# A planned GNN and mixture-of-experts kernel: layer 3's batch statistics three tiles later, layer 2's PSUM copies on ScalarE, and slack in the planner behind TensorE's products

## The chip, the cores and the metric

The kernel runs on one core of one Trainium2 chip. The metric is the device time of one execution in microseconds, as the median of three runs. A profile is one further execution, recorded by the hardware profiler. The engines are named TensorE (PE, and PEld for its weight loads), VectorE (DVE), ScalarE (ACT), GpSimd (POOL) and SyncE (SP, which issues DMAs). Each engine has its own queue of instructions and takes them in order, so an instruction that waits holds up everything behind it on that engine.

## The reference, cut to what matters

The input x has 3125 nodes with 256 features; 50,000 edges are sorted by their target node. Four times a graph layer and a feed-forward layer are added to x, each on a layer norm of x. The change touches the layers with index 2 and 3.

```python
# layer 2, graph: attention over the edges into a node
z = h @ W_func.T                       # e from z[src], z[dst], w; softmax over a node's edges
h_new = h @ W_self.T + segment_sum(alpha[:, None] * z[edge_src], edge_dst)
out = h + relu(where(deg > 0, h_new, h))
# layer 2, feed-forward: 16 experts, 256 -> 512 -> 256, the best two for each node
topk_vals, topk_idx = top_k(x @ gate_w + gate_b, 2)
moe = sum(softmax(topk_vals) * expert_out[topk_idx]);  layer norm of x + moe
# layer 3, graph: maximum over the edges (and the node itself), then batch norm
xp  = relu(x @ W_proj.T + b_proj)
agg = segment_max(xp[src], dst)
out = relu(agg @ W_l.T + b_l + x @ W_r.T)
mean, var = out.mean(axis=0), out.var(axis=0)   # over all 3125 nodes
out = (out - mean) * rsqrt(var + 1e-5) * gamma + beta
# layer 3, feed-forward: 8 experts, 256 -> 512 -> 256, the best two for each node
```

## The kernel before, in words

All is float32. Nodes lie in 25 tiles of 128 rows, sorted so that tile 0 holds the nodes with most incoming edges; tile t needs RND[t] rounds (line 70: 32, 24, 22, ... down to 9, in all 413), and in each round every one of its nodes takes one neighbour. A round is one indirect DMA on GpSimd's queue (`gather`, line 136), which fetches 128 rows of a table in HBM by index. Routed rows go back to HBM with an indirect DMA of the same kind (`scatter`, line 140).

**Layer 2** runs in one stretch whose order is not the order of the code. Several Python generators ("chains") each yield their next step as (engine, estimated us, what it needs); class `Plan` (line 1693) keeps an estimated time at which each engine is free, and always issues the step that can start first, by rank where several are within 0.05 us. A step's result counts as there after its estimate and a delay of its engine (TensorE 0.35, VectorE 0.13, ScalarE 0.2, GpSimd 2.4 us). Where a step names two engines, the one that can start first takes it, ScalarE on a tie. The plan fixes the order of instructions on each engine for good; on the chip semaphores alone decide when each starts. The chains are:

- `gathers` (line 2214): per tile one gather of the tile's own rows (XX) and RND[t] of neighbour rows (g_rows, blocks of 4 rows, 9 blocks in a ring).
- `attend` (2229): per tile a transpose and a product pu on TensorE (one PSUM buffer), a copy a_xt on ScalarE, on VectorE the scores g_e, on ScalarE their exponential (2261), on VectorE the sum g_dn and its reciprocal (2263 to 2266), the first accumulation with pu (2268), and one multiply-add for each gathered row (2273), which frees the block.
- `route2` (2281): for six groups of tiles the layer norm (ScalarE), a transpose and a copy r_xt (`logit_steps`, 1818, from `turned_steps`, 1761: either engine), the router's product and its sum r_lg on VectorE (1832), then `Experts.route` (1883): the best two, counts by a product (1904), positions, two scatters per tile to xg, and the experts' output bias as a product from a copied ro_ct (1969) added to a base row in ACC (1976).
- `tokens`, `weights` (1988, 2000): SyncE's loads of an expert's rows and its weights, two buffers each.
- `experts2` (2290), which runs `Experts.run` (2021) for three chunks of tiles (CH2, line 76: tiles 15 to 24, 6 to 14, 0 to 5), 16 experts each, at the lowest rank: rows are transposed and copied from PSUM as ro_xt (2045, either engine), multiplied with W1 (1982), passed through the activation to ro_h on ScalarE (2063), multiplied with W2 (1986), and copied from PSUM as ro_y (2080, either engine).

The first `pl.run` (2338) ends when all groups are routed. Then the remaining experts run beside `fetch` and `table3` (2294), which combine the experts' rows, norm them and write layer 3's table tab3.

**Layer 3's graph part** has an order written by hand (from line 2388). GpSimd's gathers run 24 rows ahead (ROWS). For each tile t, TensorE transposes x to g_xt (copied by ScalarE, line 1653); VectorE takes RND[t] maxima into ACC (2395), and after each issues the gather of the row 24 further on; then TensorE transposes the result (g_at, copied by ScalarE), two pairs of products (2405, 2407) give the two halves of the tile's output, and ScalarE's Relu puts them into Y (2408). Two `bn_stats` on VectorE (`stats`, 2384) take a tile's contribution to the batch norm:

```python
if t and r == OFF[t] + 6:
    stats(t - 1)
```

that is, the statistics of the tile before stand behind the seventh maximum of the present tile, and those of the last tile behind the loop. Layer 3's feed-forward part is planned again, in the manner of layer 2, with its own `Experts`.

Of the kernel before, what the change touches and what calls it, by code (L numbers as in the profile page):

```python
# [21 lines left out]
NT = 25  # L22
# [15 lines left out]
GT = 5  # L38
MM_COL = 0.0019
# [31 lines left out]
OFF = [sum(RND[:t]) for t in range(NT + 1)]  # L71
# [24 lines left out]
def tile_gnn_ffn(ctx: ExitStack, tc: tile.TileContext, a: dict, out: bass.AP):  # L96
# [1686 lines left out]
    plan = [None]  # L1783
# [34 lines left out]
    def logit_steps(lg, src, g, w, b, n, ready, R, pool, name, us, *args, **kw):  # L1818

        last = None  # L1820
        for i in range(g + 1):
            if i < g:
                xt = pool.tile([P, 2, P], F32, name=name, bufs=2)
                xf = yield from turned_steps(R["tp"], xt, src[:, i, :], ready[i], us, *args, **kw)
            if i:
                f = yield "PE", 0.4, (last[1], R["u"])
                free = R["u"].take()
                pl_ = ps("u", [P, 2, D])[:, 0, :n]
                for k in range(2):
                    nc.tensor.matmul(pl_, last[0][:, k, :], w[:, k, :], start=(k == 0), stop=(k == 1))  # L1830
                f = yield "DVE", 0.08, (f,)
                nc.vector.tensor_add(lg[:, i - 1, :], pl_, b)
                free.t = f
            last = (xt, xf)
        return f
# [8 lines left out]
    class Experts:  # L1844
# [3 lines left out]
        def __init__(self, key, n, act, chunks, pool, xg, yg, scale=None, bias=None):  # L1848
            self.n, self.act, self.chunks, self.pool, self.xg, self.yg = n, act, chunks, pool, xg, yg
            self.scale, self.bias = scale, bias  # L1850
# [32 lines left out]
        def route(self, c, t0, g, lg, f, residual, R, pre="ro_"):  # L1883
# [25 lines left out]
            f = yield "DVE", 0.16, (f,)  # L1909
# [44 lines left out]
            there = f  # L1954
            last = None
            for t in range(t0, t0 + g):
# [10 lines left out]
                f = yield ("ACT", "DVE"), 0.25, (f,)  # L1967
# [7 lines left out]
                f = yield "DVE", 0.33, (f,)  # L1975
# [45 lines left out]
        def run(self, c, R):  # L2021
# [4 lines left out]
            def turn(e):  # L2026
# [5 lines left out]
                for q in range(2):  # L2032
                    f = yield "PE", 0.13 * k, (xl, R["tp"])
                    free = R["tp"].take()
                    pt = ps("tp", [P, 512])
                    for i in range(k):
                        nc.tensor.transpose(pt[:, i * m : (i + 1) * m], x[:, i, q * P : (q + 1) * P], ident[:m, :m])  # L2037
                    if q:
                        xfree.t = f
                    f = yield ("ACT" if self.scale is not None else ("ACT", "DVE")), 0.15 + cols * 0.0011, (f,)  # L2040
                    if self.scale is not None:
                        nc.scalar.activation(xt[:, q, :], pt[:, :cols], AF.Identity, bias=self.bias[:, q : q + 1],  # L2042
                                             scale=self.scale[:, q : q + 1])
                    else:
                        (nc.scalar.copy if plan[0].on == "ACT" else nc.vector.tensor_copy)(xt[:, q, :], pt[:, :cols])
                    free.t = f
# [3 lines left out]
            for e in range(self.n):  # L2050
# [18 lines left out]
                for i0 in range(0, k, 2):  # L2069
# [9 lines left out]
                    f = yield ("ACT", "DVE"), 0.15 + 0.27 * g, (f,)  # L2079
# [70 lines left out]
    with tc.tile_pool(name="g2", bufs=2) as gp, \  # L2150
# [130 lines left out]
        def route2():  # L2281
            for c, t0, g in ((0, 20, 5), (0, 15, 5), (1, 10, 5), (1, 6, 4), (2, 0, 4), (2, 4, 2)):
                s = slice(t0, t0 + g)
                ready = yield from norm_steps(XN[:, s, :], X[:, s, :], g, gp, "rn_", [done[t] for t in range(t0, t0 + g)])
                lg = wp.tile([P, GT, 16], F32, name="r_lg")
                f = yield from logit_steps(lg, XN[:, s, :], g, rw2, gb2, 16, ready, R, gp, "r_xt", 0.36, which=("ACT", "DVE"))
# [43 lines left out]
        with tc.manual_schedule(engines={EN.PE, EN.DVE, EN.Activation, EN.Pool, EN.SP}):  # L2330
# [5 lines left out]
                                   .rearrange("p r d -> p (r d)"), here[order2[-1]])))  # L2336
            last = pl.add(4, experts2())
            pl.run(moved, R.values())
            ex2.rest(range(NT))
# [11 lines left out]
    with tc.tile_pool(name="w3", bufs=1) as wp:  # L2351
# [9 lines left out]
        with tc.tile_pool(name="g3", bufs=2) as gp, psums(tp=3, mm=4):  # L2361
# [25 lines left out]
            with tc.manual_schedule(engines={EN.PE, EN.DVE, EN.Activation, EN.Pool, EN.SP}):  # L2387
                for r in range(ROWS):
                    look(r)
                for t in range(NT):  # L2390
# [3 lines left out]
                    for r in range(OFF[t], OFF[t + 1]):  # L2394
                        nc.vector.tensor_tensor(u, u, rows.pop(r), op=OP.max)  # L2395
                        look(r + ROWS)
                        if t and r == OFF[t] + 6:
                            stats(t - 1)
# [10 lines left out]
                stats(NT - 1)  # L2409
# [131 lines left out]
```

## Time and profile before

| What | us |
|---|---|
| median of 3 runs (4182.8 to 4201.5) | 4183.03 |
| the profiled execution's own time | 4229.5 |
| its span, first to last instruction | 4227.7 |
| layers 0 and 1, up to layer 2's first gather | 0 to 2074 |
| layer 2's gathers, attention, routing and experts | 2074 to 2940 |
| layer 2's last experts, norms and tab3 | 2940 to 3179 |
| layer 3's gathers, maxima and statistics | 3179 to 3784 |
| layer 3's feed-forward part | 3784 to 4228 |
| TensorE, VectorE, ScalarE, GpSimd busy in the whole span | 2697.7, 1946.6, 845.3, 1758.5 |

Stages are cut by hand where the instructions of the next begin; all times inside the span are of the one profiled execution. Busy time is the sum of the instructions' records. "Waited for" puts the idle time in front of an instruction down to the event that ended it: an instruction, a DMA, "issue" where the profile shows nothing that was waited for, "remote" where the source is not known. A tile's name stands without buffer numbers: `ro_xt<-tp` is the copy that fills ro_xt from PSUM's tp.

### The profile page before, as it was taken

The numbers are of one execution on the slowest core, as the hardware profiler recorded it, in microseconds if no ns is written. First come the engines' busy times: TensorE is split into PE (matmuls) and PEld (weight loads), VectorE is DVE, ScalarE is ACT, GpSimd is POOL, SyncE is SP. The second block draws the span as 40 slices with busy tenths as digits, with TensorE's granted clock in tenths as the row PEclk, the third lists the DMA queues.
The fourth block names the chain that finished last, engine by engine and source line by source line (L and its number), as shares of the span: only waits on it lengthen the run. The fifth ranks groups of instructions, "written<-read, shape, count | busy, mean of one in ns | idle before, by whom it ended". The sixth has DMA issues, their size and how long they took to land. (4 is left out here: it accounts for less than half of the span.)

```text
span 4227.7 us, 46661 instructions
## 1 busy us (share of the span) xinstructions
PE 2697.7 (64%) x12940; PEld 2134.4 (50%) x12940; DVE 1946.6 (46%) x7501; ACT 845.3 (20%) x1803; POOL 1758.5 (42%) x1996
## 2 busy tenths in 40 slices
PE   1688999989889999948411365365670112137875
PEld 0566878767677878737310254254550111125653
DVE  3445666665665555442344333444662233245300
ACT  1112232221122222211100021122220000013322
POOL 4342333341253333002466544544437666643323
PEclk9878999999799999968755576577775555566987
DMA  7766455452243444113233254365523333323543
GB/s 223 223 190 187 129 157 144 130 154 65 76 118 107 118 133 126 52 48 107 73 93 91 86 175 141 107 185 168 174 90 101 87 92 88 92 81 107 158 159 100
DMA packets 275971, 521.46 MB, mean 123 GB/s; under 512 B 53609, under 2 KB 176897, under 8 KB 275685
## 3 DMA queue, kind: packets, MB, share of 16 engines
q0 software_dynamic: 105344, 306.57, 25.0%
q1 hardware_dynamic: 159598, 201.27, 15.6%
q10 hardware_dynamic: 10742, 10.34, 0.8%
q8 instruction: 114, 1.87, 0.2%
q14 instruction: 173, 1.41, 0.1%
HBM read 431.19 MB, written 86.78 MB: 123 GB/s over the span
## 5 line engine op out<-in xcount | busy, mean ns | idle before, releaser
L136 POOL DMA_INDIRECT g<-tab,m_si x521 | 498.0, 956 | 989.9 <-DVE mt L890 526.5
L136 POOL DMA_INDIRECT g_rows<-tab,srcI x413 | 401.9, 973 | 300.4 <-DVE ACC L2273 157.3
L136 POOL DMA_INDIRECT g_row<-tab,srcI x413 | 400.4, 970 | 196.3 <-issue 104.6
L880 PEld LDWEIGHTS c<-s,g 128*128 128x128 f32 x2084 | 345.8, 217 | 166.7 <-issue 83.9
L880 PE MATMUL c<-s,g 128*128 128x96 f32 x2084 | 356.1, 299 | 100.1 <-issue 38.2
L887 PE MATMUL pw<-w_d,f 65*128 65x256 f32 x1042 | 374.4, 445 | 14.2 <-DVE mt L890 11.9
L919 PE MATMUL f<-w_rel,aT 128*126 128x256 f32 x1600 | 372.6, 383 | 0.1
L884 ACT COPY aT<-c 128x384 f32<-128x384 f32 (+1 forms) x323 | 237.1, 737 | 595.7 <-PE c L880 397.5
L1982 PE MATMUL mm<-ro_xt,ro_w 128*128 128x192 f32 (+3 forms) x928 | 255.9, 428 | 122.3 <-ACT ro_h L2063 73.1
L919 PEld LDWEIGHTS f<-w_rel,aT 128*126 128x126 f32 x1600 | 300.2, 190 | 50.5 <-issue 5.3
L1651 PE MATMUL tp<-ident,ACC 128*128 128x128 f32 x50 | 16.1, 424 | 462.5 <-DVE ACC L2395 357.2
L890 DVE TENSOR_TENSOR mt<-pw,g 128x256 f32<-128x256 f32 x521 | 218.7, 420 | 159.0 <-PE pw L887 83.8
L1986 PE MATMUL y<-ro_w,ro_h 128*96 128x256 f32 (+2 forms) x1040 | 263.6, 409 | 33.5 <-ACT ro_h L2063 19.1
L1982 PEld LDWEIGHTS mm<-ro_xt,ro_w 128*128 128x128 f32 x928 | 183.8, 221 | 178.4 <-ACT ro_h L2063 80.5
L1651 PEld LDWEIGHTS tp<-ident,ACC 128*128 128x128 f32 x50 | 7.1, 199 | 470.5 <-issue 441.1
L1986 PEld LDWEIGHTS y<-ro_w,ro_h 128*96 128x96 f32 (+2 forms) x1040 | 190.4, 189 | 86.9 <-ACT ro_h L2063 23.1
L1037 PE MATMUL w<-w,b_h 128*126 128x256 f32 x800 | 218.5, 398 | 11.1 <-ACT xt L950 3.0
L1028 PE MATMUL w<-xt,w 128*128 128x252 f32 (+1 forms) x832 | 221.3, 392 | 6.3 <-issue 3.4
L140 POOL DMA_INDIRECT xg<-XX,ro_pos x100 | 101.6, 1016 | 287.6 <-issue 136.5
L2273 DVE SCALAR_TENSOR_TENSOR ACC<-g_rows,g_e,ACC 128x256 f32<-128x256 f32 x413 | 200.9, 486 | 43.9 <-DVE ACC L2273 19.9
L2395 DVE TENSOR_TENSOR ACC<-ACC,g_row 128x256 f32<-128x256 f32 x413 | 173.2, 424 | 67.1 <-DMA g_row<-tab,srcI 48.0
L2240 PE MATMUL pu<-w_s,a_xt 128*128 128x256 f32 x100 | 45.9, 606 | 231.5 <-DVE ACC L2268 104.8
(580 smaller groups left out, 4791.0 us busy)
## 6 DMA issues: line engine op xcount, KB each, us to landing
ro_w<-in_L_ffn_blocks SPq DMA_DIRECT2D x58, 514.0 KB
ro_w<-in_L_ffn_blocks SPq DMA_DIRECT2D x58, 512.0 KB
f<-in_attr_t SPq DMA_DIRECT2D x521, 32.5 KB
xg<-zero SPq DMA_DIRECT2D x78, 200.0 KB
b_at<-in_edge_attr SPq DMA_DIRECT2D x100, 125.0 KB
tabr<-v SPq DMA_DIRECT2D x12, 758.0 KB
g<-tab,m_si POOLq DMA_INDIRECT x521
g_rows<-in_L_ffn_blocks SPq DMA_DIRECT2D x14, 514.0 KB
```

The costliest lines, as they stand in the source:

```text
L136: return nc.gpsimd.indirect_dma_start(out=dst, out_offset=None, in_=table, in_offset=bass.IndirectOffsetOnAxis(ap=idx, axis=0))
L880: nc.tensor.matmul(pc[:, h, o : o + GW], g[:, h * P : (h + 1) * P], sums[k][0], start=True, stop=True)
L884: nc.scalar.copy(aT[:, :, :, b : b + n * GN].rearrange("p k r n -> p k n r"), pc[:, :, : n * GW].rearrange("p k (n r) -> p k n r", r=16))
L887: nc.tensor.matmul(pw, feats.pop(k), wd, start=True, stop=True)
L890: nc.vector.tensor_tensor(mt[0], pw, rows.pop(k)[:, D:], op=OP.mult)
L919: nc.tensor.matmul(cur["f"][:TN], aT[:, h, r, :], wrel[:, h, r, :], start=(r == 0 and h == 0), stop=(r == 15 and h == 1))
L1028: nc.tensor.matmul(ph, w["01"][:, e, k, i * P : (i + 1) * P], xt[:, k, : n * TN], start=(k == 0), stop=(k == 1))
L1037: nc.tensor.matmul(py, last[:, k, i * TN : (i + 1) * TN], w["02"][:, e - 1, k, :], start=(k == 0), stop=(k == 1))
L1982: nc.tensor.matmul(ph, w[:, o : o + P], xt[:, k, :], start=(k == 0), stop=(k == 1))
L1986: nc.tensor.matmul(py, h[:, i, s], w[:, i * D : (i + 1) * D], start=(i == 0), stop=(i == self.fc - 1))
L2273: stt(u, g[:, r, :D], e[:, r0 + r : r0 + r + 1], u, op0=OP.mult, op1=OP.add)
L2395: nc.vector.tensor_tensor(u, u, rows.pop(r), op=OP.max)
```

## The change

It has four parts. In layer 3 the statistics of tile t - 3 (LATE) take the place of those of tile t - 1, and those of the last three tiles stand behind the loop. In layer 2, while the first plan runs, `Experts.out` is ScalarE alone, so the copies ro_xt, ro_ct and ro_y that either engine could take have only ScalarE; after that plan both are allowed again. The copies r_xt of layer 2's router are ScalarE's alone too, through the default of `turned_steps`. And for the groups of chunks 0 and 1 the planner counts 3 us more (SLACK) until a product of TensorE is there for a VectorE step of the routing (the sum r_lg, the positions, the base rows), and 1.5 us more before the scatters; the yielded steps themselves are unchanged. No arithmetic is added or taken away.

```diff
--- before.py
+++ after.py
@@ -36,6 +36,8 @@
 ROWS = 24
 W_BUFS = 2
 GT = 5
+LATE = 3
+SLACK = 3.0
 MM_COL = 0.0019
 KEEP = max(1, N // 2) - 1
 KB = -(-KEEP // P)
@@ -1780,7 +1782,7 @@
         free.t = f
         return f
 
-    plan = [None]
+    plan, slack = [None], [0.0]
 
     def norm_steps(dst, src, n, pool, pre, ready, twice=False, which=("ACT",)):
 
@@ -1828,7 +1830,7 @@
                 pl_ = ps("u", [P, 2, D])[:, 0, :n]
                 for k in range(2):
                     nc.tensor.matmul(pl_, last[0][:, k, :], w[:, k, :], start=(k == 0), stop=(k == 1))
-                f = yield "DVE", 0.08, (f,)
+                f = yield "DVE", 0.08, (f + slack[0],)
                 nc.vector.tensor_add(lg[:, i - 1, :], pl_, b)
                 free.t = f
             last = (xt, xf)
@@ -1847,6 +1849,7 @@
 
         def __init__(self, key, n, act, chunks, pool, xg, yg, scale=None, bias=None):
             self.n, self.act, self.chunks, self.pool, self.xg, self.yg = n, act, chunks, pool, xg, yg
+            self.out = "ACT", "DVE"
             self.scale, self.bias = scale, bias
             self.f, self.fc, self.blocks = 512, 512 // P, a[key + "_blocks"]
             self.b2 = pool.tile([n, D], F32, name="ro_b2")
@@ -1906,7 +1909,7 @@
             at, sofar = small_("at", [GT, n])[:, :g], self.sofar[c]
             run = small_("run", [GT, n])
             pm = pm.rearrange("p k (t e) -> p k t e", e=n)
-            f = yield "DVE", 0.16, (f,)
+            f = yield "DVE", 0.16, (f + slack[0],)
             nc.vector.tensor_tensor(at[:, 0, :], pm[:, 0, 0, :], sofar, op=OP.add)
             nc.vector.tensor_tensor(run[:, 0, :], pm[:, 1, 0, :], sofar, op=OP.add)
             for i in range(1, g):
@@ -1951,7 +1954,7 @@
             for us in (0.26, 0.26, 0.26, 0.26, 0.08, 0.08, 0.26):
                 f = yield "DVE", us, (f,)
                 next(steps)
-            there = f
+            there = f + slack[0] / 2
             last = None
             for t in range(t0, t0 + g):
                 h = NV if t == NT - 1 else P
@@ -1964,7 +1967,7 @@
                 free = R["tp"].take()
                 pt = ps("tp", [P, 512])[:n, :P]
                 nc.tensor.transpose(pt, comb[:, t - t0, :], ident)
-                f = yield ("ACT", "DVE"), 0.25, (f,)
+                f = yield self.out, 0.25, (f,)
                 ct = pool.tile([n, P], F32, name=pre + "ct", bufs=2)
                 (nc.scalar.copy if plan[0].on == "ACT" else nc.vector.tensor_copy)(ct, pt)
                 free.t = f
@@ -1972,7 +1975,7 @@
                 free = R["u"].take()
                 py = ps("u", [P, 2, D])[:, 0, :]
                 nc.tensor.matmul(py, ct, self.b2, start=True, stop=True)
-                f = yield "DVE", 0.33, (f,)
+                f = yield "DVE", 0.33, (f + slack[0],)
                 nc.vector.tensor_add(ACC[:, t, :], py, residual[:, t, :])
                 free.t = self.placed[t].t = f
 
@@ -2037,7 +2040,7 @@
                         nc.tensor.transpose(pt[:, i * m : (i + 1) * m], x[:, i, q * P : (q + 1) * P], ident[:m, :m])
                     if q:
                         xfree.t = f
-                    f = yield ("ACT" if self.scale is not None else ("ACT", "DVE")), 0.15 + cols * 0.0011, (f,)
+                    f = yield ("ACT" if self.scale is not None else self.out), 0.15 + cols * 0.0011, (f,)
                     if self.scale is not None:
                         nc.scalar.activation(xt[:, q, :], pt[:, :cols], AF.Identity, bias=self.bias[:, q : q + 1],
                                              scale=self.scale[:, q : q + 1])
@@ -2076,7 +2079,7 @@
                         self.out_of(py[:, i, :], w2, h, slice((i0 + i) * m, (i0 + i + 1) * m))
                     if i0 + g == k:
                         free2.t = f
-                    f = yield ("ACT", "DVE"), 0.15 + 0.27 * g, (f,)
+                    f = yield self.out, 0.15 + 0.27 * g, (f,)
                     (nc.scalar.copy if plan[0].on == "ACT" else nc.vector.tensor_copy)(y[:, i0 : i0 + g, :], py)
                     free.t = f
                 r0 = e * cols
@@ -2281,9 +2284,10 @@
         def route2():
             for c, t0, g in ((0, 20, 5), (0, 15, 5), (1, 10, 5), (1, 6, 4), (2, 0, 4), (2, 4, 2)):
                 s = slice(t0, t0 + g)
+                slack[0] = SLACK if c < 2 else 0.0
                 ready = yield from norm_steps(XN[:, s, :], X[:, s, :], g, gp, "rn_", [done[t] for t in range(t0, t0 + g)])
                 lg = wp.tile([P, GT, 16], F32, name="r_lg")
-                f = yield from logit_steps(lg, XN[:, s, :], g, rw2, gb2, 16, ready, R, gp, "r_xt", 0.36, which=("ACT", "DVE"))
+                f = yield from logit_steps(lg, XN[:, s, :], g, rw2, gb2, 16, ready, R, gp, "r_xt", 0.36)
                 yield from ex2.route(c, t0, g, lg[:, :g], f, XN, R)
             moved.t = f
 
@@ -2334,8 +2338,10 @@
             pl.add(0, ex2.tokens())
             pl.add(0, ex2.weights((blocks, lambda: gp.tile([P, GB, ZW], F32, name="g_rows", bufs=GR_BUFS)
                                    .rearrange("p r d -> p (r d)"), here[order2[-1]])))
+            ex2.out = "ACT"
             last = pl.add(4, experts2())
             pl.run(moved, R.values())
+            ex2.out = "ACT", "DVE"
             ex2.rest(range(NT))
             pl.meet(6.0)
             last[0] = 0
@@ -2394,8 +2400,8 @@
                     for r in range(OFF[t], OFF[t + 1]):
                         nc.vector.tensor_tensor(u, u, rows.pop(r), op=OP.max)
                         look(r + ROWS)
-                        if t and r == OFF[t] + 6:
-                            stats(t - 1)
+                        if t >= LATE and r == OFF[t] + 6:
+                            stats(t - LATE)
                     at = gp.tile([P, 2, P], F32, name="g_at")
                     turned(at, u)
                     for i in range(2):
@@ -2406,7 +2412,8 @@
                         for k in range(2):
                             nc.tensor.matmul(py, wl[:, k, o], at[:, k, :], start=False, stop=(k == 1))
                         nc.scalar.activation(Y[:, i, t * P : (t + 1) * P], py, AF.Relu, bias=bl[:, i : i + 1])
-                stats(NT - 1)
+                for t in range(NT - LATE, NT):
+                    stats(t)
 
 
         mv = wp.tile([P, 2, 2], F32, name="c_mv")
```

## The prediction

> **What bounds the kernel now.** I read the page, then the busy time by stage (queried for the stages that the diff touches), then who waited for whom on GpSimd, VectorE and ScalarE in those stages, and last the order of single instructions. The columns of the stage table are stretch, length, and busy us of PE, PEld, DVE, ACT and POOL with their counts, then clock, DMA share, GB/s.
>
> ```profile
> 2074.00:2390.00 316.00, 64.29 (x178) 39.84 (x179) 148.65 (x500) 24.28 (x67) 191.80 (x213) 0.50 0.32 87
> 2390.00:2940.00 550.00, 303.48 (x1294) 236.28 (x1293) 203.02 (x644) 99.87 (x257) 277.99 (x302) 0.70 0.50 150
> ...
> 3179.00:3784.00 605.00, 111.58 (x498) 99.39 (x498) 187.13 (x478) 35.23 (x99) 400.42 (x413) 0.54 0.31 90
> ```
>
> No engine is full in them. GpSimd is the busiest but for the middle one, and it runs one row gather after the other; a gather's record lasts 0.95 us and the next follows 0.30 us later, so the undisturbed step is 1.25 us. Layer 3's 413 gathers start between 3179.3 and 3769.0: 589.7 us for 412 steps, 1.43 each. At 1.25 they would take 515.0. So **74.7 us of this stage are waits of GpSimd**, and the waits by releaser (us in total, times, longest) say on whom:
>
> ```profile
> POOL g_row L136 <- issue: 104.6, 319, 6.1
> POOL g_row L136 <- DVE ACC L2395: 87.9, 86, 10.7
> ```
>
> Nearly all of the first is the 0.30 us step; the second is a row buffer that VectorE's max (L2395) has not yet freed. VectorE is busy for 187 of 605 us and still late, because of this:
>
> ```profile
> DVE c_bs L2384 <- issue: 184.7, 15, 22.9
> DVE c_bs L2384 <- ACT c_y L2408: 173.0, 21, 25.5
> ```
>
> ```profile
> 3229.77 0.43 DVE L2395 TENSOR_TENSOR ACC<-ACC,g_row 128x256 f32<-128x256 f32 x1 [0.86 <-DMA g_row<-tab,srcI]
> 3230.11 0.29 DVE L2384 BATCH_NORM_STATS2 c_bs<-c_y 128x6 f32<-128x128 f32 x1
> 3247.14 0.29 DVE L2384 BATCH_NORM_STATS2 c_bs<-c_y 128x6 f32<-128x128 f32 x1 [16.74 <-issue]
> 3247.35 9.00 DVE L2395 TENSOR_TENSOR ACC<-ACC,g_row 128x256 f32<-128x256 f32 x20
> ```
>
> The reader sees VectorE stand for 16.74 us in front of the second statistic of tile 0 while rows land, and then do 20 maxes in a row. The statistic waits for ScalarE's Relu, and that for TensorE:
>
> ```profile
> 3246.74 0.37 ACT L2408 ACTIVATE c_y<-mm,c_bl 128x128 f32<-128x128 f32 x1 [20.76 <-remote]
> ```
>
> The last matmul for this Relu starts at 3225.5, and the Relu only at 3246.7. In this stage a product that TensorE shows as done is released up to 22 us late (the longest wait of a Relu is 22.0). I do not know why; I use only that it is so.
>
> In layer 2's stage (2074.7, first gather, to 2939.1, last) GpSimd's gaps over 1.6 us sum to 260 us; its waits:
>
> ```profile
> POOL g_rows L136 <- DVE ACC L2273: 157.3, 22, 29.6
> ...
> POOL xg L140 <- issue: 87.7, 38, 35.4
> POOL g_rows L136 <- DVE r_lg L1832: 24.6, 2, 18.3
> ```
>
> 182 us are gathers whose buffer VectorE holds, 78 us scatters of routed rows whose indices are late. VectorE (2390 to 2940) in turn stands here:
>
> ```profile
> DVE ro_xt L2045 <- remote: 105.6, 5, 29.1
> DVE ro_xt L2045 <- PE tp L2037: 90.8, 6, 27.8
> DVE r_xt L1773 <- PE tp L1768: 40.1, 5, 22.2
> DVE g_dn L2263 <- ACT g_e L2261: 20.3, 8, 8.9
> ```
>
> With 15.7 and 7.7 from two smaller rows, the copies of expert tokens (ro_xt) cost VectorE 219.8 us and the copies for the router (r_xt) 40.1: 260 us in front of copies of 0.35 us each. So VectorE holds GpSimd in both stages, not by its work but by the place of a few instructions that wait for TensorE.
>
> **The change, part by part.** *Layer 3's statistics.* No instruction is added; 50 statistics stay. Tile t's pair now stands behind the seventh row of tile t+3. From tile t's last max to there lie two tiles and seven rows; the shortest case (11+10+7 rows, at the end) is 28 x 1.25 = 35 us. A Relu comes at worst 22 us late, the second of a tile up to 39 us after its tile's transposed copy (3258.6 to 3297.8, with one lag behind the other). 24 row buffers give GpSimd another 30 us before it notices. So I take all 74.7 us. What is late next is the end: last gather to last statistic is 13.6 us now (3769.0 to 3782.6). After, it is 2.8 to land (3179.3 to 3182.1), 0.4 for the max, 3.1 to the Relu's end (as now, 3778.8 to 3781.9), and six statistics in place of two: 6 x 0.29 = 1.7. That is 8.0, a gain of 5.6. But the last products may lag: nothing to 39 us; I take 10, half of one usual lag, as the last tiles come 11 us apart, closer than most. Term: 74.7 + 5.6 - 10 = **70** (41 to 80).
>
> One rule speaks against this. The Trainium skill, "SBUF — State Buffer", section "Who interferes with whom", says that VectorE and GpSimd share a port pair under an exclusive lock, where the loser blocks for the whole instruction. By it each gather would also pay for one 0.42 us max: 412 x 1.67 = 688 us, an estimate that makes the stage 98 us longer. The trace decides otherwise: between 3200 and 3230, one max per gather, the gather lasts 0.95 us; beside 20 maxes in a row it lasts 1.07. The sum goes without it.
>
> *Layer 2's copies.* By the order of instructions, 21 ro_xt, 12 r_xt and 3 ro_ct copies leave VectorE for ScalarE inside the stage; the expert rows of the title (ro_y) were all on ScalarE already in layer 2, so that part alone is worth nothing. ScalarE is busy for 100 of 550 us, and 36 copies of 0.31 to 0.37 us (12 us) find room. What counts is the queue: behind each copy on ScalarE stands, once per tile, the exponential g_e (L2261), and VectorE's g_dn waits for it. Bounds: none of the 260 us returns and GpSimd's 182 us go, or all returns and nothing goes. The nearest row is g_dn's own, 20.3 us in 8 waits. I expect each of the 12 tiles in this stretch to wait as long as a ro_xt copy now does (219.8/21 = 10.5 us): 126 us return, about half, and half of 182 is 91. Since 32 experts run beside 12 exponentials, 2.7 per tile, I take two thirds of that: **60** (0 to 182).
>
> *Slack of 3 us in the planner.* It changes estimates, not work: router sums, positions and base rows move behind rows of the next tile on VectorE, and by the order of instructions GpSimd does 9, 13 and 32 more gathers before the scatters of the first three groups. These wait 16.8, 35.4 and 13.5 us now; 9 x 1.25 = 11, 13 x 1.25 = 16, and all of the 13.5 are filled: **41** (0 to 66). The fourth group stays where it was, and so do chunk 1's start and the end of the stage: 128 Relus of experts stand before the last exponential in both orders. The last tiles and all of layer 3's experts have no slack and keep their order. If GpSimd runs ahead, its cover is 9 blocks of 4 rows, 45 us; once they are used up, a wait on VectorE counts in full.
>
> Sum: 70 + 60 + 41 = 171 us. The profiled execution took 4229.5 us (span 4227.7), 1.1% over the median of 4183.03. So 4058.5 there, and by the same ratio (0.9596) **4014 us** for the median. That the profiled run is only 46 us longer than the others shows that the 335 us of waits cannot all be made by profiling.
>
> **Rivals.**
> A, the forecast: all of layer 3, part of layer 2, 4014 (3960 to 4075). For it: VectorE's waits stand at the moved instructions by name. Chance 0.52.
> B, layer 2 gives nothing, because ScalarE waits for the same late products (ro_h 112.3 + 37.4, ro_y 82.8 + 38.0 + 32.2 us in this stretch) and the exponentials queue behind them. Only 70 us go: 4114 (4085 to 4150). Against it: the first exponential of the expert phase now stands ahead of the first copies. Chance 0.23.
> C, TensorE is freed too: its weight loads stand 225 us in front of pu (L2240), whose one buffer VectorE frees (L2268); if that ends, GpSimd runs through: 80 + 182 + 66 = 328 at most, some 270 likely: 3916. Chance 0.13.
> D, slower: the exponentials on ScalarE. If each of the 24 tiles' exponentials stands behind copies for longer than VectorE stood at them, layer 2 loses. To pass 0.5% above before it has to lose 70 + 21 = 91 us in GpSimd's gaps, 7.6 us more per tile over the 12 tiles than today's 260 us of copy waits, and that after the 45 us of cover. A ro_y wait of 17.9 or a ro_h wait of 12.3 in front of each would do it: 12 x 15 = 180 lost, less 70 and 41: 4250. Chance 0.07.
> E, the change does not do what it says: layer 3's maxes become late for another reason (ScalarE's order copy, Relu, Relu, copy lags by over three tiles) and the statistics stall as now: 4170 to 4200. Chance 0.05.
>
> **How the numbers follow.** Range 3925 to 4135: it takes in A, B but for its end, and most of C; left out are some 0.06 of C and B and the 0.12 of D and E. A change within 0.5% (21 us, about what a measurement of this kernel can tell from none) is E. Faster: A, B and C, 0.88; same 0.05; slower 0.07.
>
> **What the changed profile would show.** Layer 3: gathers from first to last in some 515 to 525 us, c_bs waiting under 20 us, GpSimd's wait for the max near nothing, though Relus may still start 20 us late. Layer 2: no ro_xt on VectorE before the last gather, the scatters' waits shorter, g_dn's wait for g_e grown from 20 to some 130 us, gathers from first to last in some 765 instead of 865 us. I am wrong if c_bs still waits, if g_dn takes over 200 us (B, D), or if layer 2's saved time comes back between the last gather and 3179, where the leftover experts run.

## The result, and the profile after

The change moved nothing that can be measured: 4200.15 us against 4196.33 for the kernel before on the same chip (20 runs each), ratio 1.0005 (95% 0.9993 to 1.0018). 4014 was forecast. The profiled execution of the changed kernel has a span of 4206.3 us.

The stages of the changed kernel (stretch, length, busy us of PE, PEld, DVE, ACT, POOL with counts, clock, DMA share, GB/s):

```profile
2067.00:2390.00 323.00, 65.33 (x180) 40.09 (x180) 148.00 (x499) 24.42 (x71) 203.57 (x226) 0.50 0.33 90
2390.00:2925.00 535.00, 293.43 (x1288) 228.00 (x1287) 192.63 (x612) 108.25 (x289) 264.48 (x289) 0.72 0.50 151
3162.00:3767.00 605.00, 100.44 (x498) 88.63 (x498) 189.11 (x490) 34.83 (x100) 395.90 (x413) 0.55 0.32 91
```

The instructions moved (ScalarE has 289 records in the second stretch, 257 before), the lengths hardly. Layer 2's gathers take 854.6 us from first to last (861.8 before), layer 3's 577.3 (589.7), and from layer 3's first gather to the first f_yn, the work behind the statistics, it is 604.8 (607.3).

Layer 3's waits after the change, by releaser (us in total, times, longest):

```profile
DVE c_bs L2390 <- ACT c_y L2414: 154.6, 15, 24.1
...
POOL g_row L138 <- issue: 113.4, 353, 6.2
DVE c_bs L2390 <- issue: 96.7, 7, 22.4
...
POOL g_row L138 <- DVE ACC L2401: 68.8, 51, 21.3
```

A statistic three tiles late still waits: 251 us in all, 358 before. GpSimd still waits 69 us for VectorE's maxes, 88 before. Why is seen on ScalarE, after the change:

```profile
3285.16 0.37 ACT L2414 ACTIVATE c_y<-mm,c_bl 128x128 f32<-128x128 f32 x1 [21.34 <-remote]
3290.77 0.37 ACT L1655 COPY g_xt<-tp 128x256 f32<-128x256 f32 x1 [5.24 <-remote]
3296.43 0.37 ACT L1655 COPY g_at<-tp 128x256 f32<-128x256 f32 x1 [5.28 <-remote]
3318.77 0.37 ACT L2414 ACTIVATE c_y<-mm,c_bl 128x128 f32<-128x128 f32 x1 [21.97 <-issue]
3341.16 0.37 ACT L2414 ACTIVATE c_y<-mm,c_bl 128x128 f32<-128x128 f32 x1 [22.02 <-issue]
```

Copy, copy, Relu, Relu, at distances of 5.6, 5.7, 22.3 and 22.4 us: 56 us a tile, while a tile has 16.5 gathers, 20.6 us, on average. Between two Relus lie 8 matmul records, between two copies 2. So TensorE takes **2.8 us for each record** here. This is worked out from the times at which ScalarE is let go on; the matmul records themselves do not show it: after the copy at 3352.43 they start 0.2 us apart and are over by 3357, while the two Relus come at 3374.76 and 3393.66. The lag is no delay that every product has once; it is TensorE's pace, and the tiles pile up until any fixed number of them is used up. GpSimd then stops:

```profile
3372.65 0.95 POOL L138 DMA_INDIRECT g_row<-tab,srcI  x1 [0.30 <-issue]
3394.95 1.01 POOL L138 DMA_INDIRECT g_row<-tab,srcI  x1 [21.35 <-DVE ACC L2401]
```

In five of the six longer pauses, the end of the gathers among them, TensorE is back at 0.1 to 0.2 us a record 3 to 7 us after the pause begins (in this one after some 17 us), works off what had piled up, and 4 to 10 us into the next gathers it is slow again.

Layer 2's waits of GpSimd and of VectorE after the change:

```profile
POOL g_rows L138 <- DVE ACC L2276: 131.9, 19, 33.1
...
POOL xg L142 <- issue: 72.8, 38, 29.0
POOL g_rows L138 <- DVE r_lg L1834: 26.3, 2, 15.4
POOL g_rows L138 <- DVE ro_t_o L277: 17.5, 2, 17.2
POOL xg L142 <- ACT ro_ct L1972: 14.7, 1, 14.7
POOL xg L142 <- ACT ro_y L2083: 12.5, 1, 12.5
```

```profile
DVE g_dn L2266 <- ACT g_e L2264: 152.8, 9, 36.9
DVE r_lg L1834 <- PE u L1832: 56.5, 8, 24.3
```

The 260 us of waits at copies left VectorE, and at these two lines its waits grew from 41 us before (20.3 + 20.4) to 209: 168 came back. GpSimd's waits in layer 2 only changed their names: the six rows above sum to 276 us, the three rows of before to 270. The scatters (xg), which the slack was to have ready sooner, wait 100 us in place of 88.

### The profile page after: what moved, and what is told of

Its sections match the earlier page's. It is cut to its first block, busy times and chain, and to the rows that moved or that the text cites. A ratio compares the mean times of both kernels' runs of the same rounds, so it can differ in the third digit from the quotient of the medians.

```text
span 4206.3 us, 46661 instructions
## 1 busy us (share of the span) xinstructions
PE 2676.6 (64%) x12940; PEld 2115.5 (50%) x12940; DVE 1934.5 (46%) x7465; ACT 853.0 (20%) x1839; POOL 1751.6 (42%) x1996
## 4 chain that ended last, share of the span: by engine, by line
PE 14%; another core or an unknown queue 13%; issue 10%; DVE 6%; POOL 3%; DMA 3%; ACT 2%; POOLq 0%; DVEq 0%; ACTq 0%
PE y L1989 5%; PE mm L1985 5%; DVE ACC L2276 2%; DMA xg<-XX,ro_pos 1%; POOL g_row L138 1%; PE tp L2040 1%; POOL ro_g L138 1%; POOL xg L142 1%; POOL g_rows L138 1%; PE u L1832 1%; DMA tab<-ACC,idI 1%; PE tp L1770 0%; PE mm L2411 0%; PE u L1977 0%
## 5 line engine op out<-in xcount | busy, mean ns | idle before, releaser
L2411 PE MATMUL mm<-g_xt,c_wr 128*128 128x128 f32 x200 | 49.5, 393 | 373.9 <-issue 205.7
L2411 PEld LDWEIGHTS mm<-g_xt,c_wr 128*128 128x128 f32 x200 | 41.0, 286 | 381.4 <-issue 208.3
L889 PEld LDWEIGHTS pw<-w_d,f 65*128 65x128 f32 x1042 | 180.2, 216 | 14.6 <-DVE mt L892 10.5
```

The lines of the kernel that those rows point to most:

```text
L889: nc.tensor.matmul(pw, feats.pop(k), wd, start=True, stop=True)
```

## The experiments

Kernels compared with each other ran on one chip beside the kernel before, whose median was 3754 us in the first group below and 4202 to 4230 in the others; a ratio is always to the kernel before beside it.

**1. All statistics behind the loop; the other work too; fewer products; plain rows.**

late_all:

```diff
-LATE = 3
+LATE = 25
```

> All statistics of layer 3 stand behind the loop, so that VectorE waits for nothing but rows. Three theories. G (the traces of before and after suggest it): while GpSimd's gathers follow one another without a pause, TensorE takes about 2.8 us for each record of a 128x128 product, against 0.1 to 0.2, and goes back to its own pace about 5 us after the gathers pause. Then the gathers take 515 to 520 us from first to last, ScalarE's second Relu of the tiles comes every 55 us up to there (9 to 11 of 25 tiles done at the last gather), the others follow at about 2.8 us a tile, and the first f_yn starts 560 to 575 us after the first gather (605 after the change): 4155 to 4170 us. F (the prediction's own: a product is released late by a fixed 22 us and the work does not pile up): gathers 515, f_yn at 525 to 535: 4115 to 4130. C (TensorE's clock is low by itself, whatever GpSimd does): the tiles left at the last gather go on at 55 us each, f_yn at 1000 or later: above 4600.

Measured: 3756.48 us, ratio 1.0014 (1.0002 to 1.0025). Here the kernel *before* took 3754 too: in this group of runs no product is slow. The Relus:

```profile
2862.26 0.37 ACT L1655 COPY g_at<-tp 128x256 f32<-128x256 f32 x1 [49.04 <-PE tp L1653]
2863.97 0.37 ACT L2414 ACTIVATE c_y<-mm,c_bl 128x128 f32<-128x128 f32 x1 [1.33 <-PE mm L2413]
2865.68 0.37 ACT L2414 ACTIVATE c_y<-mm,c_bl 128x128 f32<-128x128 f32 x1 [1.34 <-PE mm L2413]
```

1.71 us from Relu to Relu, 0.21 a record, at a granted clock of 0.5; layer 3's gathers take 515.7 us, layer 2's 607.8. So the same program has two paces, some 440 us apart, and the one with slow records is what the prediction's profile showed. The record has the same chip number, 13, for this group and for groups 2 and 3, where records are slow; so a difference between chips is not shown, and where texts here speak of a chip's property, a state of one chip would do as well. None of the three theories was tested here, but the change's layer 2 part was: all of it is in this kernel, and with layer 3's statistics behind the loop it gained nothing where nothing is late.

dense_after:

```diff
-(in the tile loop) xt, at, products, Relu; stats(t - LATE)
+(in a second loop behind it) xt, at, products, Relu, stats(t)
```

> All of TensorE's and ScalarE's work of layer 3 stands behind the gathers and maxes. G: gathers 515 to 520 us from first to last, then 25 tiles at 2.8 us, first f_yn 585 to 595 us after the first gather: 4185 to 4195 us, nearly the time after the change, since it gives back as dense work what the pauses cost. F: the same 585 to 595. C: 25 tiles at 55 us, above 5000 us.

Measured: 3756.15, ratio 1.0000 (0.9988 to 1.0013); f_yn 532.7 us after the first gather. The edit did not do what the expectation says: the order on TensorE and ScalarE is the same in one loop or two, and they wait for the maxes alone, so their work was not postponed. It equals late_all.

no_wr:

```diff
-turned(xt, XN[:, t, :])
-nc.tensor.matmul(py, wr[:, k, o], xt[:, k, :], start=(k == 0), stop=False)
-nc.tensor.matmul(py, wl[:, k, o], at[:, k, :], start=False, stop=(k == 1))
+nc.tensor.matmul(py, wl[:, k, o], at[:, k, :], start=(k == 0), stop=(k == 1))
```

> Leaves out the x W_r term of layer 3 with its two transposes: 10 records of TensorE to a tile in place of 20. G with a price to each record: 28 us a tile while gathers run (8 records of 2.8 between the transposed copy and the second Relu's two halves of 11 us), against 20 us of gathers, so that the lag grows slowly: gathers 525 to 550 us from first to last. F: a Relu still 22 us late whatever the number of products, gathers 515. If slow spells start only where TensorE's burst is long enough to raise its granted clock to 1.0 (in the trace after the change each spell begins at such a rise), the shorter burst may never start one: Relus within 2 us of the products, gathers 515, no granted clock of 1.0 before the last gather.

Measured once, 3748 us, f_yn after 526.9: with no slow products nothing is told; it is run again in group 3.

plain_rows:

```diff
-gather(rows[r], tab3, srcI[:, r : r + 1])
+nc.sync.dma_start(rows[r], tab3[(r % 24) * P : (r % 24 + 1) * P, :])
```

> Leaves out the choice of rows: each of the 413 gathers is a plain copy of 128 rows in order, 128 KB as before, issued by SyncE, and GpSimd does nothing in the loop. G as GpSimd's own doing: second Relus within 3 us of the products, no tile at 55 us. If it is the rows' traffic into SBUF that slows TensorE: Relus 22 us apart as before as long as rows come at 100 GB/s. C: 22 us apart too, and also after the last row.

Measured once, 3439 us; no Relu late, as in its neighbours. It is run again next.

**2. The same where records are slow.**

before_again:

> The kernel before, unchanged, for a second profile. In the call before this one it took 3754 us on that call's chip, where none of TensorE's products in the traces was late by over 2.5 us, against 4196 beside the change. Two theories of the 440 us. S (slow products are a property of a chip or its state): where products keep to 0.1 to 0.2 us a record, layer 2's gathers take about 607 us from first to last and layer 3's 515 to 520, in before too; where they are slow, 864 and 590. K (the kernels of that call were faster for their own edits): no, since the kernel before beside them was as fast; so S is expected, and the profile only shows which kind of chip this call has.

Measured: span 4238.0, layer 2's gathers 871.1, layer 3's 584.2, f_yn after 612.7: S in so far as the slow records are there again without any edit; whether it is the chip or its state is not told.

after_again:

> The changed kernel, unchanged. On a chip without slow products the statistics have nothing to wait for in before either (a second Relu is late by about 2 us, not 22): the change then gains what before still loses there, 0 to 10 us in layer 3 and 0 to 10 in layer 2: a ratio of 0.996 to 1.002. On a chip with slow products: 1.000 as measured beside the change, with layer 3's Relus 22 us apart.

Measured: 4237.02, ratio 1.0020 (1.0005 to 1.0034); f_yn after 605.7, layer 2's gathers 875.3. No gain again.

late_all_b:

> All statistics of layer 3 behind the loop, once more, since on the last chip no product was slow. Without slow products: as there, 515.7 us of gathers and f_yn 533 us after the first gather. With them, G (slow only while gathers follow one another): gathers 515 to 520, 9 to 11 tiles done at the last gather, the rest at 2.8 us each, f_yn at 560 to 575: 30 to 45 us less than before. C (slow whatever GpSimd does): the rest at 55 us each, f_yn above 1000.

Measured: 4256.01, **slower**, ratio 1.0061 (1.0041 to 1.0082). ScalarE around the last gather, at 3747.7:

```profile
3745.32 0.37 ACT L2414 ACTIVATE c_y<-mm,c_bl 128x128 f32<-128x128 f32 x1 [22.11 <-issue]
3767.03 0.37 ACT L2414 ACTIVATE c_y<-mm,c_bl 128x128 f32<-128x128 f32 x1 [21.35 <-remote]
...
3776.47 0.37 ACT L2414 ACTIVATE c_y<-mm,c_bl 128x128 f32<-128x128 f32 x1 [1.31 <-PE mm L2413]
3778.18 0.37 ACT L2414 ACTIVATE c_y<-mm,c_bl 128x128 f32<-128x128 f32 x1 [1.34 <-PE mm L2413]
```

Without any wait of VectorE there is no pause, and every tile takes 56 us up to the last gather: 9 of 25 are done. Then GpSimd is quiet, 24 us later TensorE is fast, and the rest follow at 2.8 us each. C is out. G has the mechanism and missed the time: the tail after the last gather is 76 us (22.6 in after_again), and the gathers are not at 515 but at 552: from 3401 on most come every 1.40 us and last 1.09 (0.95 before), in step with VectorE's maxes, also every 1.40. Which of the two sets that pace the trace does not tell. The waits that the change meant to remove were the time in which TensorE caught up.

plain_rows_b:

> Leaves out the choice of rows in layer 3: 128 rows in order by SyncE's queue in place of each gather. Without slow products: as on the last chip, f_yn 210 to 220 us after the first of layer 3's rows. With slow products, G: no Relu 22 us apart in layer 3, since GpSimd issues nothing there. If the rows' traffic slows TensorE, or if the slow gear has nothing to do with the gathers: Relus 22 us apart, 55 us a tile, and 25 tiles up to 1375 us.

Measured once: 3855.8 us; from Relu to Relu 1.71 us at most in all 25 tiles, though rows now come at 128 KB each 0.5 us. Not the rows' traffic, but what GpSimd does.

**3. The change in its two parts, shorter bursts, fewer products.**

l2_only:

```diff
-LATE = 3
+LATE = 1
```

> The change without its layer 3 part: the statistics stand one tile late as before. The prediction had 101 us for the two parts left in (copies by ScalarE alone 60, slack 41). G: on a chip with slow products the gathers of layer 2 stay at 862 to 875 us from first to last, since it is TensorE's records that are late and not who copies them: ratio 0.997 to 1.004. The prediction's terms: 0.976. Without slow products layer 2's gathers are at 607 with the change (610 for GpSimd alone at 1.25 us each would be 516 + its scatters), so at most a few us either way.

Measured: 4242.74, ratio 1.0034 (1.0015 to 1.0053), so this part costs some 0.3% here; gathers of layer 2 873.7 us; g_dn waits 152.3 us for g_e.

l3_only:

> The kernel before with its layer 3 statistics three tiles late, and nothing else. The prediction's term: 70 us, ratio 0.983. G on a chip with slow products: the first f_yn 605 us after the first gather in place of 607 to 613, ratio 0.997 to 1.001: VectorE's pauses move and shrink by the two tiles that they may now lag, about 5 us in all, and the chain after the last gather grows. Without slow products: a Relu is 2 us late, no statistics wait in before either, ratio 0.999 to 1.001.

Measured: 4229.70, ratio 1.0002 (0.9983 to 1.0022); f_yn after 605.2 us. VectorE's waits in layer 3, first before_again, then l3_only:

```profile
DVE c_bs L2384 <- issue: 197.7, 18, 24.7
DVE c_bs L2384 <- ACT c_y L2408: 153.2, 18, 22.5
DVE ACC L2395 <- DMA g_row<-tab,srcI: 57.9, 58, 10.1
```

```profile
DVE c_bs L2384 <- ACT c_y L2408: 159.0, 18, 24.6
DVE ACC L2395 <- DMA g_row<-tab,srcI: 127.1, 141, 10.1
DVE c_bs L2384 <- issue: 100.3, 6, 22.4
```

92 us less at statistics and 69 more at rows that have not come: the wait changed its name, and 7.5 us of the stage are left as gain.

spread:

```diff
-(after the tile's maxes) copies by ScalarE, 20 records in a burst
+(after a quarter of the next tile's maxes each) copy by VectorE, 4 records
```

> Layer 3's products for a tile in four portions of 4 records, each behind a copy from PSUM that VectorE makes after a quarter of the next tile's maxes (2 rows or more apart), in place of one burst of 20 records; statistics three tiles late as in the change. On a chip with slow products (G, shown by late_all_b and plain_rows_b: about 2.8 us a record while GpSimd's gathers follow one another): theory G1, every record is slow then, whatever the burst: 55 us a tile still, VectorE's copies now wait for TensorE as well, so the same time as the change or up to 40 us slower. Theory G2, a slow spell starts only where a burst is dense enough (in the traces each begins in a burst of 16 records or more, and between 2080 and 2390 us, where bursts are shorter, none begins): no Relu late by over 3 us, gathers 515 to 525 us, f_yn 530 to 540 us after the first gather in place of 605: 60 to 75 us less than before. Without slow products on this chip: as late_all there, within 5 us.

Measured: 4239.13, ratio 1.0025 (1.0001 to 1.0048). The stage with its clock (sixth figure after the length), and its Relus:

```profile
3191.00:3790.00 599.00, 136.70 (x474) 103.61 (x474) 206.25 (x549) 17.17 (x47) 398.73 (x413) 0.50 0.31 91
```

```profile
3258.75 0.37 ACT L2415 ACTIVATE c_y<-mm,c_bl 128x128 f32<-128x128 f32 x1 [14.74 <-issue]
3292.28 0.37 ACT L2415 ACTIVATE c_y<-mm,c_bl 128x128 f32<-128x128 f32 x1 [33.17 <-issue]
3314.68 0.37 ACT L2415 ACTIVATE c_y<-mm,c_bl 128x128 f32<-128x128 f32 x1 [22.03 <-remote]
```

G2 falls: bursts are short, the granted clock is 0.50 in the whole stage, and slow spells come all the same. In them Relus are 22 to 34 us apart, between them mostly 3 to 7, and VectorE stands 286 us in front of its copies g_xt. The expectation's remark that no spell begins between 2080 and 2390 us does not hold for VectorE, as its steps at 2326 us further below show.

no_wr_b:

> Leaves out the x W_r term of layer 3 with its two transposes, once more, since on the chip of its first run no product was slow (f_yn 527 us after the first gather there). With slow products and a price to each record (G1): 10 records, 28 us a tile, Relus 11 us apart; 25 tiles need 700 us at that price against 516 of gathers, so pauses remain, f_yn 540 to 570 us after the first gather. With a price only to dense bursts (G2): the burst of 8 records may be too short to start a slow spell, f_yn 525 to 535.

Measured once: 4232.5 us, f_yn after 598.1. Neither time. For 11 tiles the Relus come within 3.1 us; from the 14th to the 20th G1's price is there:

```profile
3666.77 0.37 ACT L1655 COPY g_at<-tp 128x256 f32<-128x256 f32 x1 [5.29 <-issue]
3677.95 0.37 ACT L2410 ACTIVATE c_y<-mm,c_bl 128x128 f32<-128x128 f32 x1 [10.80 <-issue]
3689.25 0.37 ACT L2410 ACTIVATE c_y<-mm,c_bl 128x128 f32<-128x128 f32 x1 [10.94 <-issue]
```

With 4 records between two Relus they are 11.2 us apart, 22.4 with 8: it is 2.8 us for each record. But the rows lag behind their gathers from long before, by 2.8 us at 3313 and by 37.5 at 3575, since now VectorE is slow:

```profile
3483.02 0.43 DVE L2399 TENSOR_TENSOR ACC<-ACC,g_row 128x256 f32<-128x256 f32 x1 [0.97 <-DVE ACC L2399]
3484.42 0.43 DVE L2399 TENSOR_TENSOR ACC<-ACC,g_row 128x256 f32<-128x256 f32 x1 [0.97 <-DVE ACC L2399]
```

One max every 1.40 us, with a row whose gather began 29 us earlier, and nothing named but the max before. After the pause at 3372 in the changed kernel the same maxes follow at 0.45. So half of TensorE's work in layer 3 is worth 8 to 15 us: the slow steps are not TensorE's alone.

**4. What in the gathers does it, and do rests help?**

no_rows:

```diff
-gather(rows[r], tab3, srcI[:, r : r + 1])
+nc.gpsimd.memset(rows[r], 0.0)
```

> Leaves out layer 3's rows: each gather is a memset of the row buffer by GpSimd, so GpSimd stays busy in a run and no transfer is issued. If the indexed transfers make the other engines slow: no Relu over 3 us after its products, VectorE's maxes at the pace of GpSimd's memsets. If GpSimd being busy does it: Relus 22 us apart as in the kernel with the change. On a chip without slow products nothing is told.

Measured once: 3816.6 us; from Relu to Relu 1.71 us at most, the last memset 207 us after the first.

gp_rows:

```diff
-gather(rows[r], tab3, srcI[:, r : r + 1])
+nc.gpsimd.dma_start(rows[r], tab3[(r % 24) * P : (r % 24 + 1) * P, :])
```

> Leaves out the choice of rows in layer 3: GpSimd issues a plain copy of 128 rows in order in place of each gather. If any transfer that GpSimd issues makes TensorE slow: Relus 22 us apart, f_yn about 605 us after the first row as with the change. If it takes the indices of the gathers: no Relu late, f_yn at 520 to 535 or sooner, as the copies allow.

Measured once: 3846.1 us, f_yn 239.5 us after the first row. No tile is slow, though GpSimd issues 413 copies in 227 us:

```profile
3200.48 0.37 ACT L1655 COPY g_at<-tp 128x256 f32<-128x256 f32 x1 [9.41 <-PE tp L1653]
3202.19 0.37 ACT L2414 ACTIVATE c_y<-mm,c_bl 128x128 f32<-128x128 f32 x1 [1.33 <-PE mm L2413]
3203.90 0.37 ACT L2414 ACTIVATE c_y<-mm,c_bl 128x128 f32<-128x128 f32 x1 [1.34 <-PE mm L2413]
```

So neither a busy GpSimd nor its plain transfers do it, but the indexed gathers. That these stages are shorter does not account for it: in the changed kernel the first Relu of layer 3 that is 22 us late starts 67 us after the first gather, and these stages last 213 to 240 us.

In the kernels with rests GpSimd writes a small SBUF tile some times after every 12th or 24th gather. The lines of rest24:

```diff
+if r % 24 == 23:
+    for _ in range(8):
+        nc.gpsimd.memset(rest, 0.0)
```

rest12:

> After each 12th gather of layer 3 GpSimd writes a small tile twice, some 1.4 us of rest from transfers, 34 times: 48 us. In layers 0 and 1 no run of gathers is longer than 13 and no product is over 6 us late. If so short a rest ends a slow spell or keeps it from starting: gathers 565 us, f_yn 580 to 585 us after the first in place of 605, 20 to 25 us less than before. If not (the recoveries seen took 4 to 24 us): the rests come on top in part, f_yn 605 to 640, 0 to 35 us slower.

Measured: 4195.13, ratio 0.9984 (0.9963 to 1.0004); f_yn after 595.3. Some spells end or don't start, others go on; 168 us of waits at statistics are left.

rest24:

> After each 24th gather GpSimd writes a small tile 8 times, some 5.7 us of rest, 17 times: 97 us. In the kernel with the change TensorE was back at its pace 4 to 7 us into five of the six pauses. If the rests end the slow spells: hardly a statistic waits, gathers 515 + 97 = 612, f_yn at 630, so 20 to 25 us slower than before. If a memset is no rest: slow spells as in the change and the rests on top, f_yn 660 or later.

Measured once: 4208.65 us, f_yn after 594.4; faster than expected, for the recoveries now leave almost no wait. VectorE's waits in layer 3:

```profile
DVE ACC L2405 <- DMA g_row<-tab,srcI: 384.4, 376, 10.2
...
DVE c_bs L2393 <- ACT c_y L2418: 2.4, 2, 2.0
```

Rests of 3.9 us do what the change was to do: statistics wait 2.4 us in all, each row is taken some 2.8 us after its gather begins. The spells are cut short, not kept away: in 10 of 25 tiles the two Relus are still 12.7 to 19.9 us apart (9 tiles at 14.0 to 22.4 in the changed kernel). And 17 rests cost about 66 us, which is what the waits had cost.

rest_l3:

> The kernel with the change, and in layer 3 after each 24th gather 6 memsets of 128x256 by GpSimd, 1.9 us, 17 times: 32 us (rest24 had 3.8 us each, no statistic waited, gathers 582, f_yn 594 us after the first gather). If 1.9 us are enough to end a slow spell: gathers 548 to 552, f_yn 560 to 570, 30 to 45 us less than the change: ratio to before 0.990 to 0.993. If they are too short: spells go on through them, statistics wait as in the change, f_yn 595 to 610: 0.997 to 1.001.

Measured: 4232.91, ratio 1.0011 (0.9995 to 1.0028); gathers 582.7, f_yn after 605.7. By the time it is the case "too short", but statistics wait only 77 us, 251 in the changed kernel. Twelve of the 17 rests last 2.2 us; in the other five GpSimd's memsets follow one another more slowly and take 3.4 to 7.7 us, so that the rests fill some 59 of the 67 us that the gathers take over 515.7. One of the five begins so:

```profile
3301.30 0.33 POOL L1844 MEMSET idle<- 128x256 f32 x1
3306.54 0.31 POOL L1844 MEMSET idle<- 128x256 f32 x1 [4.91 <-remote]
```

rest_both:

```diff
 gather(g[:, r, :], tab2, ...)
+count[0] += 1
+if count[0] % 24 == 0:
+    rest(11)
```

> As rest_l3, and in layer 2 after each 24th of its 413 gathers 11 memsets, 3.4 us, 17 times: 58 us of GpSimd's time in layer 2, the order of all else as it was. Without slow products layer 2's gathers took 607 us from first to last on the chip of late_all, with them 848 to 875. If the spells hold layer 2 as they hold layer 3 and the rests end them: 665 to 760 us, 90 to 200 less: ratio 0.945 to 0.97 with layer 3's part. If layer 2 is held by something else, the rests come on top or hide in its waits: 850 to 930, ratio 0.99 to 1.01.

Measured: 4163.15 us, ratio **0.9838** (0.9811 to 0.9866), 64 us less than the kernel before beside it, all from layer 2: its gathers take 804.8 us, 866.4 in rest_l3, though 17 rests of 4.0 us (68 us) are in them; layer 3 is as in rest_l3 (f_yn after 605.9). That is less than expected, but it beats both kernels. GpSimd's waits in layer 2, first rest_l3, then rest_both:

```profile
POOL g_rows L138 <- DVE ACC L2281: 136.5, 17, 33.0
...
POOL xg L142 <- issue: 77.5, 37, 29.4
```

```profile
POOL g_rows L138 <- DVE ACC L2286: 64.5, 9, 19.1
POOL xg L142 <- issue: 45.9, 47, 16.8
```

## Why the prediction was wrong, step by step

- **"VectorE holds GpSimd ... by the place of a few instructions that wait for TensorE"**: right as a reading of the waits, wrong as a cause. The place decides only at which instruction the wait is seen. late_all_b takes every statistic out of the way and is 0.6% slower.
- **Layer 3's term, 70 us. This is the step that failed**: "A Relu comes at worst 22 us late, the second of a tile up to 39 us after its tile's transposed copy", covered by 35 us and more. It took a pace for a fixed delay. The trace of before had it: Relus at 3246.74 and 3281.05 with two copies between, and 22 us for each 8 records. Against 20.6 us of gathers the 56 us of a tile leave a debt of 35 us per tile, and three tiles of cover are gone by the fourth. Measured in place of the 70: l3_only 1.0002 (0.9983 to 1.0022), 2 to 8 us in the profiles.
- **The rule that was rejected** was rightly rejected: where no engine is slow, gathers keep their 1.25 us beside one max each (515.7 us in late_all). The Trainium skill, "SBUF — State Buffer", section "Who interferes with whom", says of VectorE's two-port modes that the loser blocks for the whole instruction; to take this for a max of two inputs was the prediction's own step.
- **Layer 2's copies, 60 us, and slack, 41**: measured together by l2_only at 1.0034 (1.0015 to 1.0053), a loss of some 14 us. The wait of g_dn for g_e grew to 152.8 us (130 expected), so the queue on ScalarE was seen rightly. What failed is "126 us return, about half" of the 260: in the changed kernel's profile 168 return at two lines alone, and GpSimd's gathers do not get shorter. The slack's "16.8, 35.4 and 13.5 us" are not filled either: the scatters wait 100 us, 88 before. Read with layer 3, it is the pace of the engines that counts and not who makes a copy; that layer 2's gathers take 608 us where no record is slow, and that rests gain here what the moved copies did not, supports this. The split between copies and slack was not tried.
- **The end of the stage**, "10, half of one usual lag": the last gather to f_yn went from 17.5 to 27.5 us, 28.5 to 22.6 in the second pair; within the scatter.
- **Rivals.** E came true in layer 3 nearly in its words (chance 0.05), and B in layer 2. E got its small chance because the copies' and Relus' distances, 55 us a tile, were not added up and set against the 20.6 us of a tile's gathers.
- **"The 335 us of waits cannot all be made by profiling"** stands neither proved nor refuted; the two paces differ by 440 us between groups of runs.

## What to carry to other kernels

Before moving a wait, add up the distances of the instruction that is waited for: if its own chain takes longer per tile than the loop (56 against 20.6 us here), no number of tiles of delay removes the wait. A row "<- remote" or "<- issue" of the same length again and again is a rate; divide it by the records between, and compare with the rate elsewhere in the trace (2.8 and 0.21). And when a wait is taken away, ask who was catching up in it.

## What the runs showed of the hardware

- In long runs of indexed gathers, 1.25 us apart, TensorE can drop from 0.1 to 0.2 us a record to 2.8, and VectorE to steps of 0.70 and 1.40 us, for operations of 128x256 as of 128x5. In the changed kernel's layer 2, on operations of 128x5 (in late_all each of these takes 0.2 us):

```profile
2326.18 0.17 DVE L203 TENSOR_SCALAR rn_q<-rn_v 128x5 int32<-128x5 int32 x1 [1.23 <-DVE rn_v L201]
2326.89 0.17 DVE L205 TENSOR_SCALAR rn_r<-rn_q 128x5 int32<-128x5 int32 x1 [0.53 <-DVE rn_q L203]
2328.29 0.17 DVE L208 SCALAR_TENSOR_TENSOR rn_q<-rn_r 128x5 f32<-128x5 f32 x1 [1.23 <-DVE rn_r L205]
2329.69 0.17 DVE L210 TENSOR_TENSOR rn_q<-rn_q,rn_v 128x5 f32<-128x5 f32 x1 [1.24 <-DVE rn_q L208]
```

- GpSimd's memsets are slow then too: in the rest of rest_l3 at 3301 they start 5.2, 0.7, 0.7 and then 0.37 us after one another, in a quick rest 0.37 throughout. 1.40 is two steps of 0.70 and 2.8 four, so one step may be common to the engines; no run here shows what it is. VectorE and GpSimd wait there for the signal of their own instruction before, so the trace does not tell whether the work or the signal is late. TensorE's time goes by the records between two signals: 5.6 us for 2, 11.2 for 4, 22.4 for 8.
- It ends some 3 to 24 us after the gathers stop. In layer 3 plain copies by SyncE or GpSimd and memsets by GpSimd in their place do not bring it about. Other stages are longer in such runs too: layer 2's first gather comes at some 2070 us against 2000, and layer 3's feed-forward part takes 440 us against 391; these were not studied.
- In one group of runs it was not there at all, and the kernel before took 3754 us against 4196 to 4230 in the others. What differs, and what starts a spell, is open; the chip number in the record is 13 in that group and in groups 2 and 3. Instruction fetches in the traces last 1.8 us at most in both kinds of run, and the granted clock does not tell: it is 0.50 in all of spread's stage, with and without slow records.
- The Trainium skill, "TensorE: Matmul & The Clock Gate", Part 1, warns that clock events on trn2 can be unreliable and that the gate has been seen stuck at a quarter for 50 us and more. These runs agree that the record of the clock does not show the pace. But a quarter would make 0.43 us of the 0.21 at half clock (an estimate from that page), not 2.8, and VectorE slows as well, so a stuck clock gate of TensorE does not explain it.
